# Exchanging the staging places of row quarters, and two reads of layer l=0, in a graph network kernel on one core

## The chip, the cores and the metric

The kernel runs on one core of one Trainium2 chip, in one launch for all 16 graphs of the input. The metric is the device time of that launch in microseconds (us); the figure given for a kernel is the median of its runs. Beside it there is one execution taken by the hardware profiler, with its own time, its span from the first to the last instruction, and a record of every instruction.

The engines are named as the profile names them: PE is TensorE's matrix unit (PEld its weight loads), DVE is VectorE, ACT is ScalarE, POOL is GpSimd, SP is SyncE, which issues almost all transfers here.

## The reference

The input is `x` (16 graphs, 1024 nodes, 128 features) and a weighted adjacency matrix `adj` (16 x 1024 x 1024), all in float32. Two blocks follow each other, each with a residual and a layer normalisation:

```python
def _L0_gnn_ref(embeddings, adjacency_matrix, cost_matrix, W, b):
    degree = adjacency_matrix.sum(axis=-1)[:, :, None]
    sum_neighbors = jnp.einsum('bid,bij->bjd', embeddings, cost_matrix) / degree
    concatenated = jnp.concatenate([embeddings, sum_neighbors], axis=-1)
    return relu(jnp.einsum('bnk,dk->bnd', concatenated, W) + b)

def _layer(nodes, adj, ws, bs, wd, bd, wn, bn, wu, bu):
    src = nodes @ ws + bs
    src_agg = jnp.einsum('bjv,bij->biv', src, _l2norm(adj, 2))
    dst = nodes @ wd + bd
    dst_agg = jnp.einsum('bjv,bji->biv', dst, _l2norm(adj, 1))
    self_rep = nodes @ wn + bn
    upd = jnp.concatenate([src_agg, self_rep, dst_agg], axis=2)
    return jnp.tanh(upd @ wu + bu)

x = _layernorm(x + _L0_gnn_ref(x, adj, adj, L0_gnn_W, L0_gnn_b), axis=-1)
x = _layernorm(x + _L1_gnn_ref(x, adj, ...), axis=-1)
```

The second block has four such layers; layers 2 and 3 also take the outputs of earlier ones as input. What matters below: every layer needs the matrix twice, once as it is with its columns normalised (`a`, for `dst_agg`) and once transposed with its rows normalised (`at`, for `src_agg`).

## The kernel before

**Tiling.** A graph's matrix is held as `a`, 128 partitions by 8 blocks by 1024 columns (4 MB, two buffers that alternate from graph to graph), and its row-normalised transpose as `at[0]` and `at[1]`, each for 512 of the rows. The products of a layer are arranged as a Strassen-like scheme on quarters of the matrix, named M1 to M4, Z11, Z12 and Z21; `T` and `Q` hold sums and differences of quarters of `a` and `at`, and `S` those of the messages `t`. The results go to PSUM banks: m1 to m4 (`A`, `Bk`, `Dk`, `Ck` in the code) and `Z0`, `Z1` for the two halves of the nodes. Every matmul uses only 64 of the 128 columns of the array. Two lists, `upper` and `lower`, one for each half of the array, are issued in turn by `aggregate` (line 1000), so that the two halves run at the same time.

**Order.** The order of instructions on every engine is the order in which the program writes them (line 1036, `manual_schedule`). What belongs beside the matmuls is written into `aggregate` in two dictionaries keyed by the step of the upper list: `events` has the reads of the PSUM banks, and `hooks` what is prepared for the next layer or the next graph. At the same step the event comes first. Calls between the message products of layer 3 hang in `between`.

**Row quarters.** The transpose of the next graph is prepared during the last layer (l=3) of the current graph. Its matrix is read a second time from memory in four quarters of 256 rows, in another layout: `load_rows_piece` (line 636) issues eight transfers for one piece. `scale_rows` (line 643) multiplies each of the quarter's eight rows blocks by the row's inverse norm `rinv` on ScalarE, one instruction of 256 columns each, and `transpose_rows` (line 649) writes it transposed into `at` on VectorE. Quarters 2 and 3 go to `at[1]`, quarters 0 and 1 to `at[0]`. Since the on-chip memory is full, quarters wait in tiles that other things have left:

- `xa`, half a quarter, filled at `spread0` (before the matmuls of layer 3),
- a buffer of `sq`, half a quarter, filled at `squares0` (also before them),
- `place(0)` and `place(1)`, each a whole quarter, which are blocks 0 to 1 and 2 to 3 of the current graph's own `a`, free once the last layer has read them (steps 7 and 15),
- a second buffer of `sq`, half a quarter, filled at step 15 (`end0`),
- `acc`, half a quarter, filled at step 18 (`acc_rows`).

Before the change quarter 0 lies in `xa` and `acc`, quarter 1 in the two `sq` buffers, quarter 2 in `place(0)` and quarter 3 in `place(1)`. The scalings are at steps 16 (quarter 2), 23 and 26 (quarter 3 in two halves), 28 (quarter 1) and after the layer (quarter 0). The transposes are at steps 22 (quarter 2), 27 (quarter 3), 30 (quarter 1) and at step 0 of the next graph's layer l=0 (quarter 0).

**The handover to the next graph.** After layer 3's last matmul `e0` gets `Z0` added (line 1007) and goes through a tanh (line 1020). The next graph's layer l=0 begins with its messages: matmuls into four banks `pt` (line 247), to which VectorE adds a bias while it writes `t` (line 698), the message sums `S` (lines 710 to 713), and the matmuls of `aggregate`: first the products of the nodes' own features into Z1 and Z0 (`z<-x_T,wm`), then `m<-a,t` in the upper list and `m<-T,S` in the lower. `load(n)` (line 265) then fetches the graph after that into the old `a`, over the two places.

**The reads in layer l=0.** At step 22 `m4_read` copies half of `Ck` twice into `e2` on ScalarE (lines 888 and 889), and `m2_read` adds `Bk` to `e0` on VectorE (line 892) and copies a half of `e0` to `e1` on ScalarE (line 893); line 910 then adds the half of m3 on VectorE. The hook of the same step lets ScalarE square two blocks of the next graph's matrix (line 322), whose sums follow on VectorE at step 27 (line 331). `last_reads` at step 26 ends the layer's second half of nodes: lines 896, 897 (ScalarE), 901, 902 and a tanh (line 1018).

```python
events = {10: m3_half, 14: m1_read, 22: m4_and_m2_read, 26: last_reads}
hooks = {5: rstd0, 7: rows0, 11: quarter0, 15: end0, 16: scale2, 18: acc_rows, 22: rows1, 23: lambda: scale3(0),
         26: lambda: scale3(1), 27: rows2, 28: scale1, 30: rows3}
```

Of the kernel before, what the change touches and what calls it, by code (L numbers as in the profile page):

```python
# [23 lines left out]
def adj_resnorm_kernel(ctx: ExitStack, tc: tile.TileContext, x, adj, w0, b0, layers, out):  # L24
# [42 lines left out]
    QB = K // NQ  # L67
# [37 lines left out]
    two = ctx.enter_context(tc.tile_pool(name="two", bufs=2))  # L105
# [522 lines left out]
    def load_rows(b, q, st):  # L628


        n = QB // len(st)
        for i, piece in enumerate(st):
            load_rows_piece(b, q, piece, i * n, n)
        return st

    def load_rows_piece(b, q, piece, k, n):
        v = adj[b, q * QB * C:(q + 1) * QB * C].rearrange("(k r) (h g j) -> h g r k j", r=C, h=NH, g=G)
        for g in range(G):
            for h in range(NH):
                nc.sync.dma_start(piece[g * C:(g + 1) * C, :, h * P:(h + 1) * P], v[h, g, :, k:k + n])  # L640
        return piece

    def scale_rows(st, q, rinv, which=range(QB)):
        n = QB // len(st)
        for k in which:
            row = st[k // n][:, k % n]
            nc.scalar.activation(row, row, AF.Copy, scale=rinv[:, q * QB + k:q * QB + k + 1])
# [24 lines left out]
    def combine_1(y):  # L672

        nc.vector.tensor_sub(y[0, 1], y[0, 1], y[0, 0])
# [179 lines left out]
    def aggregate(b, l, feats, msgs, wm, a, at, T, Q, fT, etag, hooks={}, pieces=1, w=None):  # L854
# [32 lines left out]
        def m4_read():  # L887
            nc.scalar.copy(e2[high], Ck[low])
            nc.scalar.copy(e2[low], Ck[low])

        def m2_read():
            nc.vector.tensor_add(e0[high], e0[high], Bk[high])
            nc.scalar.copy(e1[low], e0[high])
# [14 lines left out]
        def m2_and_half_of_m3():  # L908
            m2_read()
            nc.vector.tensor_add(e0[high], e0[high], e1[high])  # L910
# [6 lines left out]
        if l == 0:  # L917
# [11 lines left out]
            ]  # L929

            def m4_and_m2_read():
                m4_read()
                m2_and_half_of_m3()

            events = {10: m3_half, 14: m1_read, 22: m4_and_m2_read, 26: last_reads}
        elif l == 1:
# [136 lines left out]
    rows, fetched = {}, []  # L1073
# [28 lines left out]
    sq = []  # L1102
# [6 lines left out]
    sq = dict(zip((4, 2, 3, 1, 0, 7, 5, 6), sq))  # L1109
# [127 lines left out]
    for b in range(B):  # L1237
        nxt = b + 1 < B
        n = b + 1
# [6 lines left out]
        if b == 0:  # L1246
# [47 lines left out]
            def folded(l, part):  # L1294
                return lambda *_: part(l, fetched[l])

            hooks = {4: lambda *_: inverses(0, st0, NB), 5: folded(2, fold_begin), 6: rows0, 7: cinv0,
                     8: folded(2, fold_end), 9: lambda *_: fold_and_scale(3, 0), 11: second0, 12: folded(3, fold_end),
                     14: lambda *_: scale_rows(rows[1], 1, rinv), 18: first0, 26: sums0}
# [5 lines left out]
        else:  # L1305
# [21 lines left out]
            def additions(*which, then=(), w=w, st=st):  # L1327
                def issue():
                    if nxt:
# [6 lines left out]
            hooks = {0: rows3, 3: weights1, 5: lambda: combine_1(yt), 7: lambda: combine(2, yt, Q),  # L1336
                     9: lambda: combine(3, yt, Q), 11: lambda: combine(4, yt, Q), 15: sums1, 20: additions(1),
                     22: additions(then=(2, 3)), 27: additions(2, 3)}
# [24 lines left out]
        hooks = {}  # L1363
        if b == 0:
            hooks = {0: sums_of(0, 1, add=(1,)), 1: lambda: combine(2, yt, Q), 2: sums_of(of=FIRST),
                     3: sums_of(2, 3, add=(2, 3)), 4: lambda: combine(3, yt, Q), 5: sums_of(4, 5, add=(4, 5)),
                     6: lambda: combine(4, y, T), 13: sums_of(6, 7), 18: lambda: combine(4, yt, Q), 19: sums_of(of=LAST),
                     22: sums_of(add=(6, 7)), 27: lambda: column_sums(n, st)}
            st = begin_sums(n)
        else:  # L1370
# [24 lines left out]
            hooks = alongside(sums_of_next, {2: begin1, 16: centre1, 19: squares1, 23: rstd1})  # L1395
        hooks = alongside(hooks, {3: weights2})
# [8 lines left out]
        hooks = alongside(hooks, {11: y4, 27: t2})  # L1405
# [49 lines left out]
        hooks, between = {4: end1} if b else {}, {}  # L1455
        if nxt:
            scales = [lambda: scale(0, 1), lambda: scale(NJ, 1), lambda: scale(0, 0), lambda: scale(NJ, 0)]
            if b == 0:
                between = {1: inverses3, 2: factors}
                hooks = {1: load_xn, 5: factors_of_rows, 7: start3, 18: factors_gathered,  # L1460
                         **dict(zip((10, 12, 14, 16), scales))}
                quarters_at = (20, 22, 25)
            else:
                between = {0: factors, 3: end1_and_load}
                hooks = {2: factors_of_rows, **dict(zip((4, 5, 7, 9), scales)), 10: factors_gathered, 16: start3}
# [8 lines left out]
        hooks = alongside(hooks, {23: weights3})  # L1474
        if b == 0:
            hooks = alongside(hooks, {8: lambda: weight_sums(own_seven(3, None))})
        aggregate(b, 2, feats, t, wm, a, at, T, Q, f23, "acc", hooks, w=p)
        wm = ahead["wm"]
        if nxt:
            yT = first_gnn(n, w["X"], w["xT"], quarters(a2), w["T2"], w["dinv"])  # L1480
            rinv = w["rinv"]
# [4 lines left out]
        hooks, between = {}, {}  # L1486
        if nxt:
            nm = f"0_{n}"
            xT2 = w["xT"]
            w = {}  # L1490
            at2 = [None, None]
            rows = {}
            y2 = quarters(a2)

            def add0(w=w):
                w["ys"] = summed(f"y0_{n}", "acc")
                for h in range(NH):
                    add_x(yT, xT2, h)

            def half_of_rows(q, i, tag, pool=one):  # L1500
                piece = pool.tile([P, QB // 2, NH * P], F32, tag=tag, name=f"rows{q}_{n}_{i}")
                rows.setdefault(q, []).append(load_rows_piece(n, q, piece, i * QB // 2, QB // 2))

            def spread0(w=w):
                norm_spread(w["ys"], yT, KS)
                half_of_rows(0, 0, "xa")

            def sum0(w=w):
                w["s"] = norm_sum(w["ys"], KS, nm)

            def centre0(w=w):
                w["sq"] = norm_centre(w["ys"], w["s"], KS, nm)

            def squares0(w=w):
                w["v"] = norm_squares(w["sq"], KS, nm)
                half_of_rows(1, 0, "sq", two)

            def rstd0(w=w, y=y, T=T):
                w["r"] = norm_rstd(w["v"], KS, nm)
                combine(4, y, T)  # L1520


            def place(i, a=a):
                return a[:, 2 * i:2 * i + 2].rearrange("p k (u c) -> p (k u) c", c=NH * P)

            def rows0():
                rows[2] = load_rows(n, 2, [place(0)])

            def quarter0(w=w):
                w["T"] = combined(n, "T")  # L1530
                combine(2, y2, w["T"])

            def end0(w=w):
                rows[3] = load_rows(n, 3, [place(1)])
                norm_end(w["ys"], w["r"], KS)
                w["x1"] = one.tile([P, N], F32, tag="xb", name=f"x1_{n}_T")
                for h in range(NH):
                    x1_features(n, w["ys"], h, w["x1"])
                w["kept"] = put_aside(n, w["ys"])
                half_of_rows(1, 1, "sq", two)  # L1540
                combine(3, y2, w["T"])

            def scale2():
                scale_rows(rows[2], 2, rinv)

            def acc_rows():
                half_of_rows(0, 1, "acc")

            def rows1(w=w):
                at2[1] = transposed(n, 1)  # L1550
                transpose_rows(rows[2], 2, at2)
                w["back"] = take_back(b, kept)

            def scale3(i):
                scale_rows(rows[3], 3, rinv, range(i * QB // 2, (i + 1) * QB // 2))

            def scale1():
                scale_rows(rows[1], 1, rinv)

            def rows2():  # L1560
                transpose_rows(rows[3], 3, at2)

            def rows3():
                at2[0] = transposed(n, 0)
                transpose_rows(rows[1], 1, at2)

            between = {0: add0, 1: spread0, 2: sum0, 3: centre0, 4: squares0}
            hooks = {5: rstd0, 7: rows0, 11: quarter0, 15: end0, 16: scale2, 18: acc_rows, 22: rows1, 23: lambda: scale3(0),
                     26: lambda: scale3(1), 27: rows2, 28: scale1, 30: rows3}
        else:  # L1570
            x1v = one.tile([P, N], F32, tag="x", name="x1_last")
            for h in range(NH):
                nc.scalar.copy(nodes(x1v[:, half(h)]), blocks(x1T[:, half(h)]))
            ident_last = one.tile([P, N], F32, tag="xa", name="ident_last")[:, :P]
            make_identity(nc, ident_last)

            def residual_last():
                o = f4[:, half(1)]
                nc.vector.tensor_add(o, o, x1v[:, half(1)])

            def transpose_last():
                pn["last"] = ps_t.tile([P, BPH, P], F32, tag="pt", name="on_1")
                for q in range(BPH):
                    i = BPH + q
                    nc.tensor.transpose(pn["last"][:, q], f4[:, i * P:(i + 1) * P], ident_last)
                stats[1] = norm_stats(pn["last"], range(BPH), f"1_{b}_1", True)

            hooks = {30: residual_last, 31: transpose_last}
# [66 lines left out]
```

## Time and profile before

| what | us |
|---|---|
| median of three runs (lowest, highest) | 2452.63 (2451.7, 2454.38) |
| the profiled execution, its span | 2452.46, 2450.7 |
| PE busy in the span | 2403.3 |
| DVE busy | 2083.5 |
| ACT busy | 975.5 |
| POOL busy | 273.5 |
| one graph to the next (the same matmul at 813.40 and 963.65 in the chain of waits) | 150.25 |
| all packets of SP's transfers, as a share of 16 DMA engines' span | 41.7% |

The span and the run's time differ by 1.8 us, which lie before the first and after the last instruction. The granted clock of TensorE is 1.0 in the whole run. In the lines of a timeline the columns are: start in us from the span's beginning, duration in us, engine, line of the program, operation, output and input by the program's names, shapes, the count of merged instructions, and in brackets how long the engine had been idle before it and what ended that. In the lines of the wait table they are the total, the number of times and the longest, in us. A matmul in float32 appears as two passes of 0.59 us each, and passes of one half of the array follow each other every 0.43 us.

### The profile page before, as it was taken

The numbers are of one execution on the slowest core, as the hardware profiler recorded it, in microseconds if no ns is written. First come the engines' busy times: TensorE is split into PE (matmuls) and PEld (weight loads), VectorE is DVE, ScalarE is ACT, GpSimd is POOL, SyncE is SP. The second block draws the span as 40 slices with busy tenths as digits, with TensorE's granted clock in tenths as the row PEclk, the third lists the DMA queues.
The fourth block names the chain that finished last, engine by engine and source line by source line (L and its number), as shares of the span: only waits on it lengthen the run. The fifth ranks groups of instructions, "written<-read, shape, count | busy, mean of one in ns | idle before, by whom it ended". The sixth has DMA issues, their size and how long they took to land.

```text
span 2450.7 us, 39040 instructions
## 1 busy us (share of the span) xinstructions
PE 2403.3 (98%) x15293; PEld 1216.4 (50%) x15293; DVE 2083.5 (85%) x2799; ACT 975.5 (40%) x1827; POOL 273.5 (11%) x102
## 2 busy tenths in 40 slices
PE   8999999999999999999999999999999999999998
PEld 4444464544645445454554635546454464544644
DVE  5898888988888888888888889888898888988854
ACT  5425334263342533435243352434425334263312
POOL 4100111101111011110111110111100111101100
PEclk9999999999999999999999999999999999999999
DMA  9527253262633527235272442624326253362400
GB/s 202 120 76 148 60 128 77 72 137 55 145 65 85 126 47 166 47 98 109 55 158 55 105 95 70 143 68 112 80 72 148 56 132 73 76 137 51 97 21 21
DMA packets 365895, 232.01 MB, mean 95 GB/s; under 512 B 152784, under 2 KB 336848, under 8 KB 365712
## 3 DMA queue, kind: packets, MB, share of 16 engines
q1 hardware_dynamic: 364944, 227.16, 41.7%
q0 software_dynamic: 768, 2.36, 0.4%
q8 instruction: 121, 1.98, 0.3%
q14 instruction: 62, 0.51, 0.1%
HBM read 209.59 MB, written 19.84 MB: 94 GB/s over the span
## 4 chain that ended last, share of the span: by engine, by line
PE 68%; DVE 15%; DMA 6%; SPq 5%; issue 3%; ACT 3%; DVEq 0%; POOLq 0%; ACTq 0%
PE m L1005 26%; PE z L1005 19%; PE pt L247 6%; PE pt_z L247 5%; PE m_f L583 5%; SPq L640 5%; DVE acc L331 2%; PE z_f L583 2%; DMA kept<-y 2%; PE pw L247 2%; DVE at L655 2%; DVE t L698 2%; DMA xk<-kept 1%; DMA a<-in_adj_dram 1%; DMA rows<-in_adj_dram 1%
## 5 line engine op out<-in xcount | busy, mean ns | idle before, releaser
L1005 PE MATMUL m<-a,t 128*64 128x512 f32 x1008 | 436.1, 595 | 11.0 <-DVE t L698 10.8
L1005 PE MATMUL m<-at,t 128*64 128x512 f32 x1008 | 417.1, 593 | 0.0
L1005 PE MATMUL m<-Q,S 128*64 128x512 f32 x880 | 394.0, 593 | 0.0
L1005 PE MATMUL m<-T,S 128*64 128x512 f32 (+1 forms) x1040 | 387.6, 573 | 1.2
L456 POOL TENSOR_TENSOR rs<-ve,mhalf 128x32 f32<-128x32 f32 x30 | 191.6, 6386 | 998.8 <-DVE ve L454 998.8
L1005 PE MATMUL z<-at,t 128*64 128x512 f32 x504 | 232.0, 593 | 0.0
L1005 PE MATMUL z<-at,S 128*64 128x512 f32 x504 | 228.3, 593 | 0.0
L1005 PE MATMUL z<-a,S 128*64 128x512 f32 x504 | 228.2, 593 | 0.0
L1005 PE MATMUL z<-a,t 128*64 128x512 f32 x504 | 226.8, 592 | 0.0
L1005 PE MATMUL z<-Q,t 128*64 128x512 f32 x504 | 226.6, 592 | 0.0
L1005 PEld LDWEIGHTS m<-a,t 128*64 128x64 f32 x1008 | 130.9, 137 | 143.3 <-issue 110.2
L1005 PEld LDWEIGHTS m<-T,S 128*64 128x64 f32 x1040 | 132.5, 137 | 136.0 <-issue 134.2
L1005 PEld LDWEIGHTS m<-at,t 128*64 128x64 f32 x1008 | 135.1, 137 | 112.5 <-issue 111.3
L1005 PE MATMUL z<-T,t 128*64 128x512 f32 x384 | 175.6, 593 | 0.0
L1005 PEld LDWEIGHTS m<-Q,S 128*64 128x64 f32 x880 | 118.2, 137 | 114.5 <-issue 113.1
L884 ACT COPY e<-m 64x512 f32<-64x512 f32 x63 | 36.6, 581 | 329.5 <-PE m L1005 329.1
L376 POOL TENSOR_TENSOR inv<-cols,mhalf 128x16 f32<-128x16 f32 (+1 forms) x17 | 46.8, 2751 | 1074.9 <-DVE cols L375 1074.9
L414 DVE TENSOR_TENSOR a<-a,cinv 128x512 f32<-128x512 f32 x250 | 154.1, 690 | 2.0 <-ACT cinv L351 1.4
L247 PE MATMUL pt<-wm,f1T 128*64 128x128 f32 (+1 forms) x1536 | 130.8, 310 | 8.8 <-ACT f1T L1018 8.8
L322 ACT ACTIVATE sq<-a 128x1024 f32<-128x1024 f32 x120 | 125.8, 1050 | 14.8 <-DVE acc L331 13.7
L906 ACT COPY e<-m 64x512 f32<-64x512 f32 x63 | 36.4, 578 | 228.0 <-PE m L1005 227.2
L317 ACT ACTIVATE a<-a 128x1024 f32<-128x1024 f32 x120 | 125.2, 1044 | 0.4
(300 smaller groups left out, 4975.5 us busy)
## 6 DMA issues: line engine op xcount, KB each, us to landing
a<-in_adj_dram SPq DMA_DIRECT2D x120, 512.0 KB, 12.3
rows<-in_adj_dram SPq DMA_DIRECT2D x480, 64.0 KB, 2.1
a<-in_adj_dram SPq DMA_DIRECT2D x240, 128.0 KB, 3.5
wm<-wsave SPq DMA_DIRECT2D x32, 704.0 KB, 5.2
wm<-wsave SPq DMA_DIRECT2D x31, 320.0 KB, 3.3
xn<-in_x_dram SPq DMA_DIRECT2D x124, 64.0 KB, 5.4
xs<-in_x_dram SPq DMA_DIRECT2D x60, 128.0 KB, 3.6
cinv<-dr SPq DMA_DIRECT2D x30, 256.0 KB, 6.3
```

Of the source, the lines that this page charges most:

```text
L247: nc.tensor.matmul(out[s], x[:, s], y, start=start, stop=stop)
L317: nc.scalar.activation(a[:, i, :], a[:, i, :], AF.Copy, accum_out=degree)
L322: nc.scalar.activation(sq, a[:, i, :], AF.Square, accum_out=state["cols"][:, i:i + 1])
L331: nc.vector.tensor_add(state["acc"], state["acc"], state[i])
L376: nc.gpsimd.tensor_tensor(inv[:, s], cols[:, s], mhalf[:, s], ALU.pow)
L414: engine.tensor_mul(a[:, i, s], a[:, i, s], cinv[:, s])
L456: nc.gpsimd.tensor_tensor(rstd, ve, mhalf[:, :n], ALU.pow)
L583: nc.tensor.matmul(o, x_, y_, start=start, stop=stop)
L640: nc.sync.dma_start(piece[g * C:(g + 1) * C, :, h * P:(h + 1) * P], v[h, g, :, k:k + n])
L655: nc.vector.transpose(at[h][:, j:j + NJ, c].rearrange("p j (k c) -> p j k c", c=C), piece.rearrange("p k (j c) -> p j k c", c=C)[:, j:j + NJ])
L698: nc.vector.tensor_add(t[j][:, o:o + 2].rearrange("p k a v c -> p k (a v c)"), pt, wm[:, 0][:, None, :].to_broadcast([P, 2, 2 * P]))
L1005: nc.tensor.matmul(o, x, y_, start=start, stop=stop)
```

## The change

It has two parts. In the last layer, the quarters exchange their places: quarter 2 goes into `xa` and the first `sq` buffer, the two that are filled ahead of the layer's matmuls; quarter 3 goes into `place(0)`, quarter 1 into `place(1)`, and quarter 0 into the second `sq` buffer and `acc`. The order of the transposes stays 2, 3, 1, 0. Quarter 2 is scaled at step 8 instead of 16, quarter 3 at step 16 instead of 23 and 26, and quarter 1 at steps 23 and 26 in two halves instead of at step 28. In layer l=0, the event at step 22 writes M2's read (lines 892, 893, 910) ahead of M4's (888, 889).

```diff
             def m4_and_m2_read():
+                m2_and_half_of_m3()
                 m4_read()
-                m2_and_half_of_m3()
...
             def spread0(w=w):
                 norm_spread(w["ys"], yT, KS)
-                half_of_rows(0, 0, "xa")
+                half_of_rows(2, 0, "xa")
...
                 w["v"] = norm_squares(w["sq"], KS, nm)
-                half_of_rows(1, 0, "sq", two)
+                half_of_rows(2, 1, "sq", two)
...
             def rows0():
-                rows[2] = load_rows(n, 2, [place(0)])
+                rows[3] = load_rows(n, 3, [place(0)])
...
             def end0(w=w):
-                rows[3] = load_rows(n, 3, [place(1)])
+                rows[1] = load_rows(n, 1, [place(1)])
...
-                half_of_rows(1, 1, "sq", two)
+                half_of_rows(0, 0, "sq", two)
                 combine(3, y2, w["T"])
...
-            def scale3(i):
-                scale_rows(rows[3], 3, rinv, range(i * QB // 2, (i + 1) * QB // 2))
-
-            def scale1():
-                scale_rows(rows[1], 1, rinv)
+            def scale3():
+                scale_rows(rows[3], 3, rinv)
+
+            def scale1(i):
+                scale_rows(rows[1], 1, rinv, range(i * QB // 2, (i + 1) * QB // 2))
...
-            hooks = {5: rstd0, 7: rows0, 11: quarter0, 15: end0, 16: scale2, 18: acc_rows, 22: rows1, 23: lambda: scale3(0),
-                     26: lambda: scale3(1), 27: rows2, 28: scale1, 30: rows3}
+            hooks = {5: rstd0, 7: rows0, 11: quarter0, 15: end0, 8: scale2, 16: scale3, 18: acc_rows, 22: rows1, 23: lambda: scale1(0),
+                     26: lambda: scale1(1), 27: rows2, 30: rows3}
```

## The prediction

> **What bounds the kernel now.** I read the page's busy table first, then TensorE's waits, then the chain of waits through one graph, and last the timelines of the engines at the two places where TensorE stops. Times are of the graph whose last layer runs from about 927 us; from graph to graph the trace repeats every 150.25 us (813.40 to 963.65 at the same matmul). The busy table:
>
> ```profile
> PE 2403.3 (98%) x15293; PEld 1216.4 (50%) x15293; DVE 2083.5 (85%) x2799; ACT 975.5 (40%) x1827; POOL 273.5 (11%) x102
> ```
>
> TensorE is the bound, so only a stop of TensorE can be won. Its two largest repeated waits (total, times, longest), and the one of VectorE that lies ahead of the first:
>
> ```profile
> PE m L1005 <- DVE t L698: 10.8, 15, 0.7
> PE pt L247 <- ACT f1T L1018: 8.8, 14, 0.6
> ```
> ```profile
> DVE at L655 <- ACT a L647: 32.5, 15, 2.4
> ```
>
> The first is the handover from one graph's last layer to the next graph's layer l=0, and the chain of waits there runs through L655, L1007 and L698. VectorE (start, duration, instruction, idle before it):
>
> ```profile
> 952.26 0.69 DVE L902 TENSOR_TENSOR e<-e 128x512 f32<-128x512 f32 x1 [0.16 <-ACT e L897]
> 955.33 2.37 DVE L655 STREAM_TRANSPOSE at<-a 128x1024 f32<-128x1024 f32 x2 [2.38 <-ACT a L647]
> 957.63 2.45 DVE L655 STREAM_TRANSPOSE at<-rows 128x512 f32<-128x512 f32 x4
> 960.00 0.65 DVE L1007 TENSOR_TENSOR e<-e,z 128x512 f32<-128x512 f32 x1
> 960.57 2.47 DVE L698 TENSOR_TENSOR t<-pt,wm 128x512 f32<-128x512 f32 x4
> 963.08 0.76 DVE L710 TENSOR_TENSOR S<-t 128x256 f32<-128x256 f32 x2
> ```
>
> Quarter 3's transposes (955.33) wait 2.38 us for ScalarE, and everything behind them is back to back. ScalarE at the same time, in two windows:
>
> ```profile
> 926.05 1.06 ACT L440 ACTIVATE sq<-y 128x1024 f32<-128x1024 f32 x1 [7.09 <-DVE y L437]
> 938.33 0.58 ACT L906 COPY e<-m 64x512 f32<-64x512 f32 x1 [11.23 <-PE m L1005]
> ```
> ```profile
> 941.27 3.30 ACT L647 ACTIVATE a<-a,rinv 128x256 f32<-128x256 f32 x8 [2.37 <-DMA a<-in_adj_dram]
> ...
> 953.61 1.69 ACT L647 ACTIVATE a<-a,rinv 128x256 f32<-128x256 f32 x4
> 955.21 3.29 ACT L647 ACTIVATE rows<-rows,rinv 128x256 f32<-128x256 f32 x8
> ```
>
> The four scalings from 953.61 are the second half of quarter 3; their end (955.30) releases VectorE. There are 11.23 us of idle ScalarE before 938.33. What TensorE sees:
>
> ```profile
> 959.61 2.17 PE L1005 MATMUL z<-x_T,wm 128*64 128x512 f32 x7
> 962.50 1.07 PE L1005 MATMUL m<-a,t 128*64 128x512 f32 x2 [0.72 <-DVE t L698]
> 963.65 0.61 PE L1005 MATMUL m<-T,S 128*64 128x512 f32 x1
> ```
>
> The reader should see more than the 0.72 us of the wait table. The two column halves of the array each take one matmul pass per 0.43 us. The z passes start at 959.31 (upper half) and 959.61 (lower); four each at that pace would let m<-a,t start at 959.31 + 4 x 0.43 = 961.03 and m<-T,S at 961.33. They start at 962.50 and 963.65 instead, because Z0 waits for L1007, t for the third L698, and S for L710. The lower half loses 963.65 - 961.33 = 2.32 us. The upper half loses less, since it got two passes done ahead: its third pass starts at 963.65 instead of 961.03 + 2 x 0.43 = 961.89, so 1.77 us.
>
> The second stop is at the end of layer l=0:
>
> ```profile
> 980.81 0.69 DVE L892 TENSOR_TENSOR e<-e,m 64x512 f32<-64x512 f32 x1
> ...
> 988.73 0.68 DVE L1007 TENSOR_TENSOR e<-e,z 128x512 f32<-128x512 f32 x1
> ```
> ```profile
> 981.04 0.58 ACT L888 COPY e<-m 64x512 f32<-64x512 f32 x1 [4.37 <-PE m L1005]
> ...
> 982.23 0.62 ACT L893 COPY e<-e 64x512 f32<-64x512 f32 x1
> ...
> 985.08 0.62 ACT L897 COPY e<-e 64x512 f32<-64x512 f32 x1
> ```
> ```profile
> 990.22 1.95 PE L247 MATMUL pt<-wm,f1T 128*64 128x256 f32 x16 [0.63 <-ACT f1T L1018]
> ```
>
> ScalarE runs without a gap from L888 at 981.04 through two squares to L897 (985.08); then L902, two L331 additions and L1007 on VectorE, the tanh on ScalarE, and TensorE's second half of pt. All of it is one chain with no slack.
>
> [...]
>
> **The change part by part.**
>
> *Loads.* Counts and order on SP stay: 8 pieces early into xa, 8 into sq, 16 into place(0) and place(1), the put_aside store, 8 into sq, 8 into acc, then take_back. Only the quarters' numbers change, so SP costs nothing. The load of the next graph (L265, issued at 957.87) overwrites place(1) and now waits for quarter 1's transposes instead of quarter 3's; these end at 957.7 (below), so it stays where it is.
>
> *Quarter 2 scaled at step 8.* Eight scalings, 3.3 us, now from the early pieces. Their second piece is issued by 927.7; with 2.1 us to landing (page, rows) they run from about 930 to 933.3, inside ScalarE's gap up to 938.33. Cost 0. If they came 5 us later they would push L906, whose result is read at 949.89 (L910): 11 us more of cover.
>
> *Quarter 3 scaled at step 16* where quarter 2 was: 941.27 to 944.6, same bytes from the same place. *Quarter 1 scaled in two halves* where quarter 3 was, ending 955.3. The eight scalings at 955.21 disappear from there.
>
> *Transposes.* At step 22 four of 128x512 (2.45 us) instead of two of 128x1024 (2.37): 0.08 us later for L892 and its followers, so quarter 1's scaling ends at 955.38. At step 27 quarter 3 has been ready since 944.6: its transposes run right after L902, 953.0 to 955.3, and the 2.38 us stall is gone. What is late next is quarter 1, ready at 955.38, just when VectorE arrives: nearly a tie, taken as 955.41. Two of 128x1024, 2.30 us as between 955.33 and 957.63: L1007 at 957.71, i.e. 2.29 us earlier. It needs Z0, whose last pass ends at 956.3; L698 needs pt, whose last bank ends at 959.77, and its fourth runs at 960.1: neither stops it. L710 comes 2.29 us earlier, so S allows 963.65 - 2.29 = 961.36, against 961.33 that the array allows. TensorE gains 2.29 us in the lower half and 1.77 in the upper; VectorE is 2.29 us earlier throughout l=0, since from 957.63 to 982 it was back to back but for one wait. Quarter 0's scaling moves with the tanh to about 959.1 to 962.4, its transposes to 963.6: covered.
>
> *L893 ahead of L888 and L889.* No instruction is added; ScalarE's copy waits for L892 (ends 980.81 + 0.69 = 981.50) while the m4 data is ready at 981.04. So 981.04 to 981.52 is lost on ScalarE, 0.48 us at the old times. VectorE's L910 comes 0.7 us earlier, which buys nothing: L896 waits for the third product, whose last pass ends at 983.6. With the new times L892 ends at 979.21, L893 runs at 979.24, the squares start at 979.24 + 1.83 = 981.07 instead of 982.87, and the chain to pt is 1.80 us earlier instead of 2.29. Cost 0.49 us per graph with a next graph, that is 14 times; the last graph has no squares there and loses nothing.
>
> *Sum.* Graphs 2 to 14: 13 x 1.80 = 23.4. Graph 1, whose handover had the same stall: 1.9. Graph 15, without squares: 2.3. Together 27.6 us. The profiled execution took 2452.46 us (span 2450.7), as the median 2452.63 within 0.01%: 2452.46 - 27.6 = 2424.9, so 2425 us.
>
> Two costs the trace doesn't show. The release of quarter 1's transposes: from 0 to +1.0 us if scaling or semaphores come later (its halves take 1.70 us each); I take 0.03. The price of L893 in front: from 0, if L892 comes 0.5 us sooner against m4, which VectorE's back-to-back row excludes nearly, to 0.6; I take 0.49.
>
> **The rivals.**
> - *The reordered copy is free.* If L892 gets ahead of m4, both are ready together and 14 x 0.49 = 6.9 us come back: 2418. For it: VectorE's lead varies with the release of its inputs. Against: L892 can't start before M2's last upper pass, which gains only 1.77 us.
> - *A new wait takes the old one's place.* Quarter 1's transposes wait about 1 us for ScalarE, or the squares of l=0 wait for the next graph's first rows. These land by 970.7 (first load to landing 5.3 us, then one about every 2.5 us) and would be wanted at 972.7 instead of 974.48. A microsecond per handover leaves 27.6 - 15 = 12.6 us: 2440.
> - *Slower.* The stall of 2.38 us is not what TensorE waits for, or returns whole on quarter 1, and L893 still stands in front: 14 x 0.49 = 6.9 us more, 2459. It decides once quarter 1's release comes 1.8 us or more after 955.4. The four times two L647 around L897 speak against it: they end at 955.30 already.
> - *The change doesn't do what it says*: only if the pieces in xa and sq were not free so early; the loads into the same tiles were issued at 919.57 without a stop before. I give it no share of its own.
>
> **How the numbers follow.** Likeliest case 0.60 (2425), copy free 0.18 (2418), new wait 0.14 (2440), slower 0.08 (2459). The range from 2416 to 2438 takes in the likeliest with its bounds, the free copy, and most of the partial wait. About 0.2% (5 us) is what a measurement here can tell from no change: faster 0.91, within it 0.03, slower 0.06.
>
> **What would show it.** Right: L655 at<-a twice in a row from 953.0 of such a graph with no wait on L647 in between; eight L647 on rows before L906; m<-T,S within 0.1 us of the pace of z; the wait of m on L698 gone from TensorE's list; L893 ahead of L888 with ScalarE idle about 0.5 us, and pt waiting 1.0 us or more for f1T instead of 0.63; a period of 148.45 us. Wrong: a wait of L655 on L647 of over 0.5 us at the second pair, squares waiting for the load of a, or a period above 149.5 us.

## The result and the profile after

The changed kernel takes 2426.86 us (median of 4 runs, 2426.72 to 2427.72) against 2452.16 us of the kernel before (median of 4, one run more than in the table of the kernel before): a ratio of 0.9896 with a 95% interval of 0.9879 to 0.9913. The profiled execution took 2427.01 us, its span is 2425.1 us. The forecast was 2425 us.

The busy table of the changed kernel:

```profile
PE 2384.9 (98%) x15293; PEld 1213.7 (50%) x15293; DVE 2084.5 (86%) x2799; ACT 977.2 (40%) x1827; POOL 273.5 (11%) x102
```

No engine does less work. Of the 25.6 us by which the span is shorter, 18.4 lay in time that the page counts as busy on TensorE, with the same 15293 passes: a stop counts as busy while one half of the array still works (before, the table of waits had 0.72 us where the lower half lost 2.32), and until the recorded end of a pass (0.59 us at a pace of 0.43). So the share stays at 98% while the time falls by 1%. The view that shows the change is TensorE's waits (total, times, longest, in us):

```profile
PE pt L247 <- ACT f1T L1018: 14.6, 14, 1.0
PE pv L252 <- DVE v L446: 6.9, 14, 0.5
```

The wait of m on L698 (10.8 us before) is gone from the list, and pt's wait for f1T has grown from 8.8 to 14.6 us. Both parts of the change are in these two facts. First the handover, VectorE's timeline in the changed kernel; the corresponding layer now ends some 8 us earlier in the run:

```profile
944.38 0.69 DVE L902 TENSOR_TENSOR e<-e 128x512 f32<-128x512 f32 x1 [0.17 <-ACT e L897]
944.99 4.84 DVE L655 STREAM_TRANSPOSE at<-a 128x1024 f32<-128x1024 f32 x4
949.76 0.65 DVE L1007 TENSOR_TENSOR e<-e,z 128x512 f32<-128x512 f32 x1
950.33 2.47 DVE L698 TENSOR_TENSOR t<-pt,wm 128x512 f32<-128x512 f32 x4
```

Between L902 and L1007 there is no idle time any more; the stall of 2.38 us stood there. The four transposes take 4.84 us where two and two would take 2.37 + 2.30: the third of them starts 0.15 us late, at 947.46, 0.03 us after quarter 1's scaling ends (945.74 + 1.69 = 947.43 in the next lines). ScalarE, where quarter 2 is now scaled from the two early pieces, ahead of L906:

```profile
918.05 1.06 ACT L440 ACTIVATE sq<-y 128x1024 f32<-128x1024 f32 x1 [7.09 <-DVE y L437]
919.01 1.69 ACT L647 ACTIVATE rows<-rows,rinv 128x256 f32<-128x256 f32 x4
921.85 1.71 ACT L647 ACTIVATE rows<-rows,rinv 128x256 f32<-128x256 f32 x4 [1.15 <-DMA rows<-in_adj_dram]
930.34 0.58 ACT L906 COPY e<-m 64x512 f32<-64x512 f32 x1 [6.78 <-PE m L1005]
...
945.74 1.69 ACT L647 ACTIVATE a<-a,rinv 128x256 f32<-128x256 f32 x4
```

The eight scalings end 6.78 us before L906 starts. TensorE at the handover:

```profile
951.31 0.59 PE L1005 MATMUL z<-x_T,wm 128*64 128x512 f32 x1
951.40 0.38 PE L247 MATMUL pt<-wm,x_T 128*64 128x256 f32 x1
951.62 1.88 PE L1005 MATMUL z<-x_T,wm 128*64 128x512 f32 x7
953.03 0.59 PE L1005 MATMUL m<-a,t 128*64 128x512 f32 x1
953.41 0.61 PE L1005 MATMUL m<-T,S 128*64 128x512 f32 x1
```

From the first z to the first m<-T,S there are 2.10 us now and were 4.34 us (959.31 to 963.65); m<-a,t follows at the pace of the array (951.31 + 4 x 0.43 = 953.03). The second place is the end of layer l=0: one line of VectorE, then ScalarE's timeline and TensorE's:

```profile
970.57 0.69 DVE L892 TENSOR_TENSOR e<-e,m 64x512 f32<-64x512 f32 x1
```
```profile
971.30 0.62 ACT L893 COPY e<-e 64x512 f32<-64x512 f32 x1 [4.45 <-DVE e L892]
971.94 0.58 ACT L888 COPY e<-m 64x512 f32<-64x512 f32 x1
...
975.35 0.61 ACT L897 COPY e<-e 64x512 f32<-64x512 f32 x1
```
```profile
980.49 1.95 PE L247 MATMUL pt<-wm,f1T 128*64 128x256 f32 x16 [1.04 <-ACT f1T L1018]
```

ScalarE is idle until L892 has ended (970.57 + 0.69 = 971.26), and pt's stop grew from 0.63 to 1.04 us. Measured against the first z of the same handover, m<-T,S starts 2.25 us earlier than before and the second half of pt 1.74 us. From graph to graph 148.51 us pass instead of 150.25.

### The profile page after: what moved, and what is told of

Read it like the earlier page. It is cut to its first block, busy times and chain, and to the rows that moved or that the text cites. A ratio compares the mean times of both kernels' runs of the same rounds, so it can differ in the third digit from the quotient of the medians.

```text
span 2425.1 us, 39279 instructions
## 1 busy us (share of the span) xinstructions
PE 2384.9 (98%) x15293; PEld 1213.7 (50%) x15293; DVE 2084.5 (86%) x2799; ACT 977.2 (40%) x1827; POOL 273.5 (11%) x102
## 4 chain that ended last, share of the span: by engine, by line
PE 55%; DVE 26%; ACT 7%; SPq 4%; DMA 4%; issue 4%; DVEq 0%; POOLq 0%; ACTq 0%
PE m L1005 20%; PE z L1005 13%; PE pt L247 6%; PE pt_z L247 5%; PE m_f L583 5%; SPq L640 4%; DVE acc L331 3%; PE z_f L583 2%; PE pw L247 2%; DVE at L655 2%; DVE t L698 2%; DMA rows<-in_adj_dram 2%; ACT a L647 2%; DVE Q L678 1%; DVE Q L680 1%
## 5 line engine op out<-in xcount | busy, mean ns | idle before, releaser
L1005 PE MATMUL m<-T,S 128*64 128x512 f32 (+1 forms) x1040 | 393.1, 573 | 0.0
L884 ACT COPY e<-m 64x512 f32<-64x512 f32 x63 | 36.6, 581 | 335.4 <-PE m L1005 334.9
L247 PE MATMUL pt<-wm,f1T 128*64 128x128 f32 (+1 forms) x1536 | 124.7, 310 | 14.6 <-ACT f1T L1018 14.6
L322 ACT ACTIVATE sq<-a 128x1024 f32<-128x1024 f32 x120 | 125.8, 1049 | 14.4 <-DVE acc L331 13.4
L247 PEld LDWEIGHTS pt<-wm,f1T 128*64 128x64 f32 x1536 | 94.3, 137 | 63.4 <-ACT f1T L1018 32.2
```

What stands on the lines that cost most here:

```text
L247: nc.tensor.matmul(out[s], x[:, s], y, start=start, stop=stop)
L322: nc.scalar.activation(sq, a[:, i, :], AF.Square, accum_out=state["cols"][:, i:i + 1])
L1005: nc.tensor.matmul(o, x, y_, start=start, stop=stop)
```

## The experiments

The theory was the prediction's: the exchange takes 2.3 us out of each handover, because quarter 3 is scaled before its turn and quarter 1 just in time; the reordered reads cost 0.5 us in each of 14 graphs. The rivals were that the order of reads is free, that it is the places as such that help, and that TensorE has slack at the handover. The runs below were taken in three rounds, each with the kernel before beside them; it took 2452.34, 2452.84 and 2452.99 us, so runs of different rounds can be compared. A period is the time from one graph to the next.

**The exchange alone** (the changed kernel with the reads put back):

```diff
             def m4_and_m2_read():
-                m2_and_half_of_m3()
                 m4_read()
+                m2_and_half_of_m3()
```

> The exchange of places and the earlier scaling alone, the reads of l=0 in their old order. My theory: the second part of the change costs 0.5 us in each of 14 graphs, so this kernel is 7 us faster than the changed one: 2420 us, period 148.0 us, TensorE waits for f1T 0.6 us instead of 1.0. Rival (the reordered copy is free, or helps since VectorE's wait at L910 is shorter): 2427 us or more.

Measured: 2418.13 us, ratio 0.986 [0.9846, 0.9873]; period 148.01 us. Its longest wait of TensorE:

```profile
PE pt L247 <- ACT f1T L1018: 8.8, 14, 0.6
```

The 0.6 us of pt are those of the kernel before. ScalarE's gap at the reads of l=0 is this:

```profile
966.86 0.58 ACT L888 COPY e<-m 64x512 f32<-64x512 f32 x1 [3.96 <-PE m L1005]
```

It was 4.45 us ahead of L893 in the changed kernel, 0.49 more. The part that was reordered costs 148.51 - 148.01 = 0.50 us a graph, and the exchange alone brings 150.25 - 148.01 = 2.24 us.

**The reads alone** (the same two lines moved in the kernel before):

> The old kernel with M2's read ahead of M4's in l=0 and nothing else. My theory: ScalarE idles 0.48 us ahead of L893 in 14 graphs and nothing later gives it back: 2459 us (6.7 us slower than before). Rival (free at the old spacing of the engines, costs only once the handover is faster): 2452 us.

Measured: 2459.18 us, ratio 1.0029 [1.0017, 1.004]; period 150.76 us, 0.51 more than before. The two parts add up: neither changes what the other does.

```profile
PE pt L247 <- ACT f1T L1018: 14.6, 14, 1.1
PE m L1005 <- DVE t L698: 10.8, 15, 0.7
```

This kernel has both waits: the handover's as before and pt's as after.

**M2's read between the two copies of M4's**, in the changed kernel:

```diff
             def m4_and_m2_read():
+                nc.scalar.copy(e2[high], Ck[low])
                 m2_and_half_of_m3()
-                m4_read()
+                nc.scalar.copy(e2[low], Ck[low])
```

> The changed kernel with M2's read between the two copies of M4's read: L888, L893, L889. My theory (the loss is ScalarE standing idle until L892 ends, and the first copy of M4 fills that time): 2420 us, as with the reads in their old order. Rival (the loss comes from L910 and L896 or from the order as such): 2424 to 2427 us.

Measured: 2417.9 us, ratio 0.9858 [0.9845, 0.9872]; period 147.90 us. In ScalarE's timeline the two copies of M4 now have lines 932 and 934:

```profile
967.88 0.58 ACT L932 COPY e<-m 64x512 f32<-64x512 f32 x1 [3.95 <-PE m L1006]
968.48 0.62 ACT L893 COPY e<-e 64x512 f32<-64x512 f32 x1
969.00 0.57 ACT L934 COPY e<-m 64x512 f32<-64x512 f32 x1
```

The first copy fills the time in which ScalarE stood idle, and the loss is gone. VectorE's L896 still waits for TensorE about as in the changed kernel (16.1 us in total against 17.7), so it was the idle time ahead of L893, not L910 and L896 or the order as such.

**Quarter 1 scaled late**, whole, behind the tanh (reads in their old order):

```diff
-            hooks = {5: rstd0, 7: rows0, 11: quarter0, 15: end0, 8: scale2, 16: scale3, 18: acc_rows, 22: rows1, 23: lambda: scale1(0),
-                     26: lambda: scale1(1), 27: rows2, 30: rows3}
+            hooks = {5: rstd0, 7: rows0, 11: quarter0, 15: end0, 8: scale2, 16: scale3, 18: acc_rows, 22: rows1,
+                     27: rows2, 28: lambda: (scale1(0), scale1(1)), 30: rows3}
```

> Places exchanged, reads in their old order, but quarter 1 scaled whole at step 28, behind the tanh. My theory (the handover waits for whichever transpose is last ready, and a microsecond of ScalarE there costs a microsecond in each of 15 handovers): quarter 1 ready 1.6 us later, a wait of L655 of 1.5 us at its second pair, 2442 us. Rival (TensorE has slack there, as the upper half gains only 1.77 of 2.29 us): 2425 us or less.

Measured: 2442.9 us, ratio 0.9959 [0.9945, 0.9972]; period 149.56 us. VectorE's timeline of this kernel:

```profile
950.88 2.37 DVE L655 STREAM_TRANSPOSE at<-a 128x1024 f32<-128x1024 f32 x2
954.95 2.37 DVE L655 STREAM_TRANSPOSE at<-a 128x1024 f32<-128x1024 f32 x2 [1.70 <-ACT a L647]
```

Quarter 3 goes at once, and quarter 1 waits 1.70 us. The period grows by 149.56 - 148.01 = 1.55 us: 1.70 less the 0.15 of the near tie. There is no slack: what the last transpose waits, every graph pays.

**The places alone, at the scaling steps of before** (reads in their old order; against the changed kernel, without the definitions of `scale3` and `scale1`, which are those of before):

```diff
-            hooks = {5: rstd0, 7: rows0, 11: quarter0, 15: end0, 8: scale2, 16: scale3, 18: acc_rows, 22: rows1, 23: lambda: scale1(0),
-                     26: lambda: scale1(1), 27: rows2, 30: rows3}
+            hooks = {5: rstd0, 7: rows0, 11: quarter0, 15: end0, 16: scale2, 18: acc_rows, 22: rows1, 23: lambda: scale3(0),
+                     26: lambda: scale3(1), 27: rows2, 28: scale1, 30: rows3}
```

> The places exchanged, but each quarter scaled at the steps of before (2 at 16, 3 in halves at 23 and 26, 1 whole at 28), the reads in their old order. My theory (what frees the handover is that quarter 3 is scaled before its turn, not where it lies): VectorE waits 2.4 us for quarter 3 as before and then about 0.9 us more for quarter 1, whose one tile is ready only after its eighth scaling: 15 x 0.85 = 13 us slower than before, 2465 us. Rival (the places themselves help, since loads and buffers come free at better times): 2452 us or less.

Measured: 2472.16 us, ratio 1.0081 [1.0066, 1.0096]. The waits came as expected, in VectorE's timeline:

```profile
659.72 2.37 DVE L655 STREAM_TRANSPOSE at<-a 128x1024 f32<-128x1024 f32 x2 [2.38 <-ACT a L647]
662.91 2.37 DVE L655 STREAM_TRANSPOSE at<-a 128x1024 f32<-128x1024 f32 x2 [0.82 <-ACT a L647]
```

Most periods are 151.19 us, 0.94 more than before; but five of the 14 are 152.4 us or more. They make up most of the 7 us more than expected and have a cause of their own, told at the end. The places alone bring a loss; what brings the gain is that the early places let quarter 2, and so quarter 3, be scaled earlier.

**One addition less ahead of L1007** (the exchange, reads in their old order). At the end of l=0 VectorE adds two squares (L331) ahead of L1007; here the second goes into the next layer:

```diff
-                     22: additions(then=(2, 3)), 27: additions(2, 3)}
+                     22: additions(then=(2, 3)), 27: additions(2)}
...
-                sums_of_next = {0: sums_of(4, 5), 1: sums_of(of=FIRST, add=(4, 5)), 2: sums_of(6, 7),
+                sums_of_next = {0: sums_of(4, add=(3,)), 1: sums_of(5, of=FIRST, add=(4, 5)), 2: sums_of(6, 7),
```

> Exchange with the reads in their old order, and of the two additions of squares ahead of L1007 in l=0 only the first stays there; the second goes to step 0 of the next layer, with the squares of block 5 behind the row sums. My theory (L1007, and with it pt's wait for f1T, stands behind VectorE's additions): the wait of 0.6 us goes, period 147.4 us, 2409 us. Rival (L1007 waits for Z0 anyway, or the moved addition is paid for in layer l=1): 2418 us or more.

Measured: 2425.84 us, ratio 0.9893 [0.9878, 0.9907]. This is a miss: slower by 7.7 us than the exchange alone. TensorE's waits:

```profile
PE pv L252 <- DVE v L446: 25.5, 14, 1.8
```

pt's wait is gone as expected, and the second half of pt starts 0.82 us earlier in the graph. But in layer l=1 VectorE now comes later to the reduction L446 of the second norm, and TensorE stands 1.8 us at the small matmul pv where it stood 0.5; the z passes written behind pv go on only after it (the last ahead of it starts at 999.26, pv at 1001.68, the next z at 1001.79):

```profile
999.26 0.59 PE L1005 MATMUL z<-at,t 128*64 128x512 f32 x1
1001.68 0.31 PE L252 MATMUL pv<-v,fold 128*64 128x32 f32 x4 [1.82 <-DVE v L446]
1001.79 0.62 PE L1005 MATMUL z<-T,t 128*64 128x512 f32 x1
```

The balance is -0.82 + 1.33 = 0.51 us a graph, and the period of 148.51 is 0.50 longer. The same split with the changed reads, and with M2's read between the copies, met the same wait:

> The changed kernel, reads in the new order, with the same split of the additions. My theory (the reordered copy costs only because L897, L902 and both additions stand in one row ahead of L1007): one addition less gives 1.2 us of room, the 0.5 us are mostly hidden, 2410 to 2413 us. Rival (the new order costs 0.5 us by itself, wherever the additions stand): 7 us above the split with the old order, 2416 us.

> The exchange, M2's read between the two copies of M4's, and the split of the additions: the best version if the readings so far hold. My theory: 2408 to 2409 us, the copies' order no longer matters. Rival: another wait takes the place of the one removed, 2414 us or more.

Measured: 2428.56 us (0.9902 [0.9886, 0.9919]) and 2425.56 us (0.989 [0.9875, 0.9904]), periods 148.58 and 148.52: both are misses too. What the reads cost can't be seen in these two, since TensorE is held at pv in both.

**pv later.** To test that cause, pv was issued at step 26 of layer l=1 instead of 23, in three of the kernels:

```diff
-            hooks = alongside(sums_of_next, {2: begin1, 16: centre1, 19: squares1, 23: rstd1})
+            hooks = alongside(sums_of_next, {2: begin1, 16: centre1, 19: squares1, 26: rstd1})
```

With the split and M2's read between the copies:

> Split additions and M2's read between M4's copies, as in the run before, and the variance sum of the second norm (pv, L252, in layer l=1) issued at step 26 instead of 23. My theory for the miss of the split (it did remove pt's wait of 0.6 us, but VectorE came to L446 1.2 us later and TensorE, in order, stood 1.8 us at pv for it): the wait at pv goes, period about 146.7 us, 2400 us. Rival (VectorE's added load in l=1 shows at its next consumer whatever the place of pv): 2412 us or more.

Without the split:

> Exchange, M2's read between M4's copies, additions as in the changed kernel, and pv at step 26. My theory: TensorE's wait of 0.5 us at pv goes in 14 graphs and the 0.5 us at pt stay: 2411 us, period 147.4 us. Rival (the 0.5 us at pv cover another stop): 2418 us.

With the split and the reads in the changed order:

> The changed kernel, reads in the new order, with the split additions and pv at step 26. My theory (the new order costs only through the row of additions ahead of L1007): within 0.2 us a graph of the same kernel with the copy in between, 2400 to 2403 us. Rival (0.5 us a graph by itself): 7 us above it.

Measured: 2397.54 us (0.9772 [0.9758, 0.9785]), 2407.26 us (0.9814 [0.98, 0.9827]) and 2397.86 us (0.9774 [0.9761, 0.9788]); periods 146.48, 147.19 and 146.55 us. The wait at pv has left TensorE's list in all three. Without the split this brings 147.90 - 147.19 = 0.71 us, a little more than the 0.5 us of the wait. With room ahead of L1007, the changed order of reads costs 146.55 - 146.48 = 0.07 us more than the order with the copy in between, where without that room it cost 148.51 - 147.90 = 0.61: its price was that it stood in one row with L897, L902 and both additions.

The first of the three is 2.3% faster than the kernel before and some 29 us faster than the changed one (2397.54 against 2426.86); the third can't be told from it. The chain of waits of this version, by engine, over the whole run:

```profile
PE 95%; DVE 2%; DMA 1%; SPq 1%; issue 1%; ACT 0%; POOLq 0%; DVEq 0%; ACTq 0%
```

It was PE 68% in the kernel before and 55% in the changed one, which is the faster of the two: the share doesn't rank kernels, but at 95% TensorE hardly waits for another engine.

## Why the prediction was right

- *The handover.* Forecast: m<-T,S 2.29 us earlier in the lower half. Measured: 2.25 us. The upper half gained 1.77 us, as forecast. VectorE kept to its order here: in the kernel before the last z pass ahead of L1007 ended at 956.32 (955.73 + 0.59), and L1007 started at 960.00, behind the transposes. The 0.04 us come from the end of quarter 1's scaling: against the first z it lies 0.13 us later than that of quarter 3 did, where the forecast had 0.08, since the four transposes at step 22 took 2.49 us and not 2.45; the release 0.03 us behind it came out. That VectorE's and TensorE's room runs out at the same moment, 961.36 against 961.33, came out: m<-T,S starts 0.38 us after m<-a,t, where the pace of the array alone would allow 0.31 (951.62 - 951.31).
- *Quarter 2's scaling at no cost.* Shown: the first four scalings run directly behind L440, earlier than forecast; then ScalarE waits 1.15 us for the second piece and has 6.78 us left before L906.
- *Nothing moved on SP.* The load of the next graph starts 1.30 us ahead of the first z (950.01 against 951.31) and did so 1.44 us ahead of it (957.87 against 959.31); in the list of ScalarE's waits the squares of l=0 (L322) wait for VectorE alone, not for a load.
- *The reads.* Forecast: 0.49 us in 14 graphs. Measured: 0.50 with the exchange, 0.51 without it. That L910's earlier time buys nothing is shown by VectorE: the 0.7 us it gained stand as a wait of 1.19 us of L896 for TensorE in the changed kernel, where the exchange alone has 0.50.
- *The sum.* Forecast 27.6 us, measured 25.3 between the medians. In the profiled executions, graphs 2 to 14 brought 1.74 each instead of 1.80, the first handover 1.74 instead of 1.9 (for which the prediction gave no working), and the last graph 2.23 instead of 2.3, together 26.6 us; against that the part before the first handover, which the change doesn't touch, was 1.04 us longer. In the profiled executions of the two kernels and of the four runs of the first round, the last z of graph 0's last layer starts between 203.1 and 205.9 us, so the 1.04 us need not be the change's.
- *The rivals.* The free copy is ruled out by the two runs that move it alone; it would have been nearly right with less work ahead of L1007. The new wait exists but measures 0.15 us. The slower case fell with the stall.

## What to carry to other kernels

Find the transfer or buffer that is ready long before its turn, and give it to whatever is needed first, so that the work on it falls into idle time; exchanging places without moving that work made this kernel slower (ratio 1.0081). A copy that waits for another engine should not stand ahead of one that is ready: the same three copies cost 0.5 us a graph in one order and nothing in another, and with an addition less behind them the order hardly mattered (0.07 us). A gain at one stop can be lost at the engine's next wait, as at pv (0.82 us gained, 1.33 lost), and here the gain showed only when that was moved as well (2425.56 to 2397.54 us).

## What was not expected of the hardware

In the kernel with the old scaling steps, the two stops of TensorE at the handover last 1.01 and 0.72 us, and behind some of them the clock of TensorE falls. The trace records six stretches of 3.41 us at half clock in this run, one in graph 0 and five at handovers, beside one at the very end. The six start at 116.24, 211.81, 515.60, 819.38, 1123.17 and 1426.95 us, that is once 95.57 and four times 303.78 or 303.79 us apart: 28 and 89 times 3.413 us (95.57/28 and 303.78/89). So these six lie on one grid. Two handovers of that kernel, cut along this grid, in the view by stretches (us from and to, then length, busy time and count of PE, PEld, DVE, ACT and POOL, granted clock, share of DMA and GB/s):

```profile
512.18:515.59 3.41, 1.68 (x6) 0.39 (x6) 3.41 (x6) 2.23 (x6) 0.00 (x0) 1.00 0.50 114
515.59:519.00 3.41, 3.41 (x9) 1.47 (x9) 3.27 (x7) 1.69 (x5) 0.00 (x0) 0.50 1.06 208
1727.33:1730.74 3.41, 1.68 (x7) 0.39 (x6) 3.41 (x6) 2.35 (x6) 0.00 (x0) 1.00 0.46 137
1730.74:1734.15 3.41, 3.33 (x16) 1.26 (x16) 3.27 (x7) 1.57 (x4) 0.00 (x0) 1.00 1.05 204
```

Behind the first stop 9 matmul passes fall into the next 3.41 us, at a granted clock of 0.50; behind the second, with the same 1.68 us of busy PE in the stretch before, 16 at full clock. A graph that is hit is about 1.3 us longer. Which stop is followed by such a stretch stays open, since the same 1.68 us were followed by both; nor do the runs show what sets the grid. In the kernel before TensorE stops for 0.72 us at the handover, without the 1.01 us, and no such stretch lies there (its only one is at the very end, with no matmul in it: granted clock 0.50 from 2449.00 to 2450.70, so the 1.0 given for its whole run is a mean); so the 0.94 us by which the period is longer here cost about 1.3 us more in five of 15 handovers.
